# One pause before w2's shift, and a longer one for the sums of single tiles, in an eight-image attention and ConvNeXt kernel

## The chip, the cores and the metric

The kernel runs on one core of a Trainium2 chip, in float32. The metric is the device time of one execution, in microseconds (us). Before the change it is 3219.33 us, the median of three runs (3218.84 to 3219.62).

## The reference: what is computed

Eight images of 384 channels and 32 x 32 pixels go through two blocks.

```python
# layer 0, tokens: (8, 1024, 384)
xn = layernorm(xf, g1, beta1)
q, k, v = split_heads(xn @ w_qkv.T + b_qkv)          # 8 heads of 48
attn = softmax((q @ k.T) * 48 ** -0.5)
x1 = (attn @ v) @ w_proj.T + b_proj + xf
h = gelu(layernorm(x1, g2, beta2) @ w_fc1.T + b_fc1) # 1536 wide, exact gelu
x = x1 + h @ w_fc2.T + b_fc2
# layer 1
y = depthwise_conv_7x7(x) + dw_b
y = layernorm(y, ln_w, ln_b) @ w1 + b1               # 1536 wide
y = gelu(y)
nx = norm_over_pixels(y) / (mean_over_channels(norm_over_pixels(y)) + 1e-6)
y = grn_gamma * (y * nx) + grn_beta + y
x = x + y @ w2 + b2
```

## The kernel before, in words

The images are worked through one after the other. Image 0 goes through layer 0; from then on an image's layer 0 is interleaved with the previous image's layer 1 (the convolution, its layer norm, its two products).

Scores and weighted values of attention are taken in steps: for each half of the queries and each of four head pairs, eight steps of four small matmuls `s` (line 818), an exponential on ACT (827), and four matmuls `o` (838). The pair of PSUM tiles `o` of a head pair is emptied by `average` (lines 772 to 805): a copy on ACT (777), an addition on VectorE (779), the sums sent by SP (783), a reciprocal on VectorE (786), two trips through memory on SP, and a multiplication on VectorE (805). The projection (760) needs all four averages of its half; the second layer norm follows it: means by TensorE (518), subtraction (561), squares on ACT (568) and their sums on VectorE (572, 575), variance by TensorE (518 again).

The larger products (q and k, fc1, fc2, w1, w2) are done with fewer matmuls, on sums and differences of blocks of the weights and of the data. For this the sums of the weights are made once, while image 0 is worked on:

- `sums_singly` (1587 to 1640) loads 15 single tiles (960 KB) by POOL into a spare part of another buffer, waits, makes 18 small sums on VectorE (14 in line 1600, two in 1603, one each in 1637 and 1638), and stores the tiles by POOL (1640). Two chains `sums_for_tiles` do this three times each, for q and k's weights, for w1 and for w1 again, with a pause of 8.0 after each; `sums_for_fc1` does it twice for fc1.
- `forms` makes the sums of larger blocks for fc2 and later for w2 (lines 1651, 1654, 1683, 1692, 1694 on VectorE, loads 1661 and stores 1669 on POOL). Its buffer has the tag `acc`.
- `shift_through_w2` (1742 to 1763) works out what the GRN's `grn_beta` adds through w2, in three rounds. Each asks POOL for two loads of w2 (1746) into the buffer with the tag `acc`, multiplies them by `grn_beta` on VectorE (1752, twice), adds them up (1755, and 1759 five times), takes the column sum by TensorE (294) and adds the bias on ACT (1763). The tile is the one that `forms("fc2")` has used, so its load comes after the last stores from there.
- `prepare(weights, False)` does `forms("fc2")`, then `shift_through_w2`, then `forms("w2")`.
- On POOL and VectorE, lines 1725 to 1730 make a similar sum for w1's shift, in `pad`.

Each engine takes its instructions in the order in which the program writes them. That order is decided by the class `Flow` (137 to 173): all side work is written as generators, which yield a pause in microseconds of TensorE work. Whenever the main loop writes matmuls it calls `flow.pe(us)`, and the chains whose pause is over write their next instructions at this point. A longer pause so moves instructions behind others in the queues of their engines; nothing waits for a time on the chip. `pause()` holds back the sums on VectorE while the list `quiet` isn't empty, which is near the end of each half of the attention. Chains that have not ended are written out whole by `flow.finish` at certain points (2095 to 2113).

fc2 (1049 to 1145) takes its products in a chain with VectorE: differences and sums of `hid` and `fc_e` (1083) feed TensorE's matmuls (496), and VectorE (1080, 1083) adds the products to `x`.

Of the kernel before, what the change touches and what calls it, by code (L numbers as in the profile page):

```python
# [176 lines left out]
def block_kernel(  # L177
# [90 lines left out]
    def col(name, i):  # L268
        at, width = VEC[name]
        assert i < width  # L270
        return vec[:, at + i : at + i + 1]
# [20 lines left out]
    def column_sums(ps, i, weights, rows=slice(0, P)):  # L292

        nc.tensor.matmul(out=ps[rows, i : i + 1], lhsT=weights, rhs=ones[:, 0:1], start=True, stop=True)
        flow.pe(0.2)
# [13 lines left out]
    def columns(name):  # L309
        at, width = VEC[name]  # L310
        return vec[:, at : at + width]
# [38 lines left out]
    def chunk(w, c):  # L350
        return w[:, c * 6 * P : (c + 1) * 6 * P]
# [1230 lines left out]
    def pause():  # L1582
        for _ in range(24):
            if quiet:
                yield 1.0

    def sums_singly(w, store, spare):

        shape = store.shape
        t = spare[:, : shape[1] * shape[2] * P].rearrange("p (g n o) -> p g n o", n=shape[2], o=P)
        nc.gpsimd.dma_start(out=t, in_=w.rearrange("p (g n o) -> p g n o", n=shape[2], o=P))
        yield 9.0
        yield from pause()
        r = {n: t[:, :, i, :] for i, n in enumerate(SINGLY)}
        a12, a13, a21, a22, a23, a31, a32, a33 = (r[n] for n in (12, 13, 9, 4, 14, 0, 3, 10))

        def plus(dst, one_, other, op=ALU.add):
            nc.vector.tensor_tensor(dst, one_, other, op)  # L1600

        def minus(dst, one_, other):
            nc.vector.scalar_tensor_tensor(dst, one_, -1.0, other, ALU.mult, ALU.subtract)

        plus(r[6], r[6], a12)
        plus(r[14], a23, a33)
        yield 0.6
        yield from pause()
        minus(r[5], r[6], a33)
        plus(r[8], r[6], a13)  # L1610
        yield 0.6
        yield from pause()
        plus(r[8], r[8], r[14], ALU.subtract)
        plus(r[11], r[14], a12, ALU.subtract)
        yield 0.6
        yield from pause()
        plus(r[13], a13, a12, ALU.subtract)
        plus(r[13], r[13], a33, ALU.subtract)
        yield 0.6
        yield from pause()  # L1620
        plus(r[7], r[14], a22, ALU.subtract)
        plus(r[4], a21, a22)
        yield 0.6
        yield from pause()
        plus(r[2], a33, r[4], ALU.subtract)
        plus(r[4], r[4], a31)
        yield 0.6
        yield from pause()
        plus(r[1], a32, r[4])
        minus(r[9], a21, a12)  # L1630
        yield 0.6
        yield from pause()
        plus(r[9], r[9], a31, ALU.subtract)
        plus(r[0], a31, r[6], ALU.subtract)
        yield 0.6
        yield from pause()
        nc.vector.tensor_scalar(r[12], a12, -1.0, None, ALU.mult)
        nc.vector.tensor_scalar(r[14], r[14], -1.0, None, ALU.mult)
        yield 1.0
        nc.gpsimd.dma_start(out=store, in_=t)  # L1640

    def prepare(weights, aside):
# [3 lines left out]
        def blocks(name):  # L1646
            t = one.tile([P, CT, N], F32, tag="acc", name=name).rearrange("p c n -> p (c n)")
            return t.rearrange("p (j k o) -> p j k o", j=4, o=P)
# [93 lines left out]
        def shift_through_w2():  # L1742
            for r in range(CT):
                t = blocks(f"w2_gbeta_{r}")
                for s in range(2):
                    nc.gpsimd.dma_start(out=t[:, s], in_=chunk(w2, 2 * r + s).rearrange("p (k o) -> p k o", o=P))
                yield 14.0
                h = HT // 2
                for s in range(2):
                    yield from pause()  # L1750
                    g = columns("gbeta")[:, s * h : (s + 1) * h].unsqueeze(2).to_broadcast((P, h, P))
                    nc.vector.tensor_tensor(t[:, s], t[:, s], g, ALU.mult)
                    yield 1.0
                yield from pause()
                nc.vector.tensor_tensor(t[:, 0], t[:, 0], t[:, 1], ALU.add)
                for k in range(1, h):
                    yield 0.5
                    yield from pause()
                    nc.vector.tensor_tensor(t[:, 0, 0, :], t[:, 0, 0, :], t[:, 0, k, :], ALU.add)
                yield 7.0  # L1760
                ps = ps_s.tile([P, N], F32, tag="s", name=f"b2_{r}")
                column_sums(ps, 0, t[:, 0, 0, :])
                nc.scalar.activation(b2[:, r : r + 1], ps[:, :1], AF.Identity, bias=col("b2", r), scale=1.0)
# [7 lines left out]
        def release():  # L1771
            yield 14.0
            weights.release()

        yield from forms("fc2", wfc2, s_fc2)
        flow.spawn(release())
        yield from shift_through_w2()
        yield from forms("w2", w2, s_w2)

# [86 lines left out]
    def main():  # L1866
# [81 lines left out]
        def sums_for_tiles(i):  # L1948
            width = len(FORMS) * P
            spare = large[0][:, (2 * NP + 2 * i) * N : (2 * NP + 2 * i + 2) * N]  # L1950
            for w, store, g in ((wqkt, s_qk, i), (w1t, s_w1, i), (w1t, s_w1, i + 2)):
                yield from sums_singly(w[:, g * width : (g + 1) * width], store[:, g : g + 1], spare)
                yield 8.0

        def sums_for_fc1():
            width = len(FORMS) * P
            spare = v.rearrange("p t w -> p (t w)")
            for g in range(2):
                yield from sums_singly(wfc1t[:, g * width : (g + 1) * width], s_fc1[:, g : g + 1], spare)
                yield 8.0  # L1960
            for t in range(KT):
                nc.gpsimd.memset(v[:, t, :], 1.0)
# [122 lines left out]
        for b in range(B):  # L2085
            if b == 0:
                folding = flow.spawn(after(None, folds(weights), 8))
                preparing = flow.spawn(after(None, prepare(weights, False), 4))
                singly = [flow.spawn(after(None, sums_for_tiles(i), 33 + 5 * i)) for i in range(2)]
                aside = flow.spawn(after(folding, prepare(weights, True), 4))  # L2090
# [4 lines left out]
            if b == 0:  # L2095
                for chain in singly:
                    flow.finish(chain)
                fc1_sums = flow.spawn(after(None, sums_for_fc1(), 22.0))
                shift = flow.spawn(after(None, prepare(weights, None), 4.0))
# [204 lines left out]
```

## Time and profile before

| what | value |
|---|---|
| median of three runs | 3219.33 us |
| the profiled execution's own time | 3214.05 us |
| its span | 3212.3 us |
| mean granted TensorE clock | 0.999 |
| TensorE busy | 3197.8 us |
| VectorE busy | 2552.1 us |
| ACT busy | 1673.5 us |
| POOL busy | 493.2 us |
| moved by DMA | 393.09 MB, mean 122 GB/s |

The span runs from the first to the last event of the profiled execution; its own time is 1.75 us longer. Busy times are those of each engine's own instructions, and engines run beside each other. In a timeline a row has the start, the duration, the engine, the line of the kernel and the operation, and in brackets how long the engine was idle ahead of it and what ended that. In a list of waits a row has the waiting engine and line, what released it, the sum, the count and the longest in us.

### The profile page before, as it was taken

The numbers are of one execution on the slowest core, as the hardware profiler recorded it, in microseconds if no ns is written. First come the engines' busy times: TensorE is split into PE (matmuls) and PEld (weight loads), VectorE is DVE, ScalarE is ACT, GpSimd is POOL, SyncE is SP. The second block draws the span as 40 slices with busy tenths as digits, with TensorE's granted clock in tenths as the row PEclk, the third lists the DMA queues.
The fourth block names the chain that finished last, engine by engine and source line by source line (L and its number), as shares of the span: only waits on it lengthen the run. The fifth ranks groups of instructions, "written<-read, shape, count | busy, mean of one in ns | idle before, by whom it ended". The sixth has DMA issues, their size and how long they took to land.

```text
span 3212.3 us, 39348 instructions
## 1 busy us (share of the span) xinstructions
PE 3197.8 (100%) x14204; PEld 1398.9 (44%) x14204; DVE 2552.1 (79%) x3587; ACT 1673.5 (52%) x2363; POOL 493.2 (15%) x592
## 2 busy tenths in 40 slices
PE   9999999999999999999999999999999999999999
PEld 5344434443444434444344443444435444344454
DVE  4447788897878978789787888788888788879964
ACT  3442663456644476444754537637365374732543
POOL 2102221112111121201112011120111201200000
PEclk9999999999999999999999999999999999999999
DMA  6525742657336564456545374463743638433244
GB/s 212 173 94 177 172 92 50 159 115 163 81 87 160 120 156 92 93 146 151 119 92 123 116 185 102 81 136 106 192 93 81 147 98 200 73 81 93 54 120 111
DMA packets 206052, 393.09 MB, mean 122 GB/s; under 512 B 42656, under 2 KB 48416, under 8 KB 205472
## 3 DMA queue, kind: packets, MB, share of 16 engines
q0 software_dynamic: 79296, 163.35, 26.6%
q1 hardware_dynamic: 126272, 226.49, 23.5%
q8 instruction: 114, 1.87, 0.2%
q10 hardware_dynamic: 288, 0.71, 0.1%
q14 instruction: 82, 0.67, 0.1%
HBM read 212.98 MB, written 40.11 MB: 79 GB/s over the span
## 4 chain that ended last, share of the span: by engine, by line
PE 95%; DMA 1%; DVE 1%; issue 0%; ACT 0%; SPq 0%; POOL 0%; DVEq 0%; ACTq 0%; POOLq 0%
PE fc L415 15%; PE s L818 13%; PE o L838 12%; PE fc_p L496 11%; PE o_p L496 11%; PE proj L760 4%; PE v L738 3%; PE h_n L467 3%; PE h_z L467 3%; PE h_x L467 3%; PE h_last L1427 2%; PE o L1378 2%; PE h L402 2%; PE qk_n L467 2%; PE qk_z L467 2%; PE qk_x L467 1%
## 5 line engine op out<-in xcount | busy, mean ns | idle before, releaser
L1244 DVE SCALAR_TENSOR_TENSOR acc<-pad,vec,acc 128x870 f32<-128x870 f32 (+8 forms) x815 | 912.3, 1161 | 2.7
L827 ACT ACTIVATE p<-s 128x1024 f32<-128x1024 f32 x512 | 523.7, 1024 | 266.6 <-PE s L818 258.3
L838 PE MATMUL o<-p,v 64*64 64x512 f32 x4096 | 540.5, 589 | 4.0 <-DVE attn L779 4.0
L818 PE MATMUL s<-qk 48*64 48x512 f32 x4096 | 542.5, 591 | 0.2 <-ACT qk L660 0.2
L1280 POOL DMA_DIRECT2D acc<-tap x266 | 226.9, 859 | 1355.0 <-ACT tap L1279 668.3
L415 PE MATMUL fc<-xn,fc 128*128 128x512 f32 x972 | 427.5, 594 | 0.0
L496 PE MATMUL o_p<-y,w 128*128 128x512 f32 x664 | 289.0, 593 | 0.0
L838 PEld LDWEIGHTS o<-p,v 64*64 64x64 f32 x4096 | 165.3, 132 | 282.4 <-issue 269.6
L415 PEld LDWEIGHTS fc<-xn,fc 128*128 128x128 f32 x972 | 183.1, 190 | 228.7 <-issue 221.5
L818 PEld LDWEIGHTS s<-qk 48*64 48x64 f32 x4096 | 161.8, 132 | 277.4 <-issue 214.8
L496 PE MATMUL fc_p<-qk,fc 128*128 128x512 f32 x520 | 226.1, 593 | 0.0
L1279 ACT ACTIVATE tap<-pad,vec 128x512 f32<-128x512 f32 x266 | 195.1, 736 | 3.2 <-DMA acc<-tap 3.1
L496 PEld LDWEIGHTS o_p<-y,w 128*128 128x128 f32 x664 | 125.6, 190 | 157.7 <-issue 146.4
L1244 DVE SCALAR_TENSOR_TENSOR acc_last<-pad,vec,acc_last 128x377 f32<-128x377 f32 (+24 forms) x288 | 177.3, 694 | 0.6
L496 PEld LDWEIGHTS fc_p<-qk,fc 128*128 128x128 f32 x520 | 98.3, 190 | 126.1 <-issue 117.1
L508 ACT ACTIVATE qk<-fc,bfc_f 128x512 f32<-128x512 f32 x90 | 61.6, 684 | 160.7 <-PE fc L415 160.7
L508 ACT ACTIVATE hid<-fc,bfc_f 128x512 f32<-128x512 f32 x72 | 49.3, 686 | 159.4 <-PE fc L415 159.4
L760 PE MATMUL proj<-attn,wproj_sb 128*128 128x512 f32 x288 | 129.0, 602 | 2.1 <-DVE attn L805 2.1
L779 DVE TENSOR_TENSOR attn<-o,attn 128x512 f32<-128x512 f32 x64 | 44.1, 689 | 104.4 <-ACT attn L777 102.9
L738 PE MATMUL v<-wv_sb,xn 128*128 128x384 f32 x384 | 126.8, 487 | 0.0
L991 ACT COPY pad<-x 128x512 f32<-128x512 f32 x42 | 26.4, 635 | 185.3 <-DVE x L1083 185.3
L738 PEld LDWEIGHTS v<-wv_sb,xn 128*128 128x128 f32 x384 | 72.5, 190 | 50.1 <-issue 3.3
(446 smaller groups left out, 4601.5 us busy)
## 6 DMA issues: line engine op xcount, KB each, us to landing
acc<-tap POOLq DMA_DIRECT2D x266, 256.0 KB, 3.6
fc<-s_fc SPq DMA_DIRECT2D x91, 256.0 KB, 4.6
w<-s_w SPq DMA_DIRECT2D x91, 256.0 KB, 2.7
w<-s_w SPq DMA_DIRECT2D x72, 320.0 KB, 4.2
fc<-in_wfc SPq DMA_DIRECT2D x54, 384.0 KB, 3.9
y<-y POOLq DMA_DIRECT2D x38, 512.0 KB, 6.7
qk<-qk POOLq DMA_DIRECT2D x30, 512.0 KB, 9.5
qk<-s_qk SPq DMA_DIRECT2D x42, 320.0 KB, 4.7
```

The costliest lines, as they stand in the source:

```text
L415: nc.tensor.matmul(out=ps, lhsT=lhsT(k), rhs=rhs(k)[:, half(h)], start=(k == 0), stop=(k == nk - 1))
L467: nc.tensor.matmul(out=at, lhsT=weights.at(wname, g, slot // 5)[:, slot % 5, :], rhs=rhs[n], start=first, stop=True, skip_group_check=not ...
L496: nc.tensor.matmul(out=bank, lhsT=lhsT, rhs=rhs, start=k == 0, stop=k == len(pairs) - 1)
L508: nc.scalar.activation(dst, src, function, **kw)
L738: nc.tensor.matmul(out=ps[:, :C], lhsT=xn[:, k, t * P : (t + 1) * P], rhs=wv_sb[:, k, :], start=(k == 0), stop=(k == CT - 1),)
L760: nc.tensor.matmul(out=ps, lhsT=wproj_sb[:, m, ct * P : (ct + 1) * P], rhs=attn[:, m, :], start=(m == 0), stop=(m == CT - 1),)
L818: nc.tensor.matmul(out=s[64 * i : 64 * i + 64, j, :], lhsT=kT[64 * j : 64 * j + HD, m, k0 : k0 + 64], rhs=qT[64 * j : 64 * j + HD, m, half ...
L827: nc.scalar.activation(p, s, AF.Exp)
L838: nc.tensor.matmul(out=outs[i][64 * j : 64 * j + 64, :], lhsT=v[keys, t, at : at + 64], rhs=p[keys, j, :], start=(t == 0), stop=(t == KT - 1),
L1244: nc.vector.scalar_tensor_tensor(dst, window, tap, dst, ALU.mult, ALU.add)
L1279: nc.scalar.mul(t.rearrange("p (h w) -> p h w", w=W), window, tap)
L1280: nc.gpsimd.dma_start(out=acc[:, ct, half(h)], in_=t, accum_op=ALU.add)
```

## The change

The pause between asking for a group of 15 single tiles and the first sum on them becomes 13.0 where it was 9.0, in all eight uses. And between `forms("fc2")` and the shift through w2 there is a pause of 8.0 where there was none; `forms("w2")`, which comes after the shift in the same chain, is written later by the same. No instruction is added or removed.

```diff
@@ -1591,7 +1591,7 @@
         nc.gpsimd.dma_start(out=t, in_=w.rearrange("p (g n o) -> p g n o", n=shape[2], o=P))
-        yield 9.0
+        yield 13.0
         yield from pause()
@@ -1774,6 +1774,7 @@
         yield from forms("fc2", wfc2, s_fc2)
         flow.spawn(release())
+        yield 8.0
         yield from shift_through_w2()
         yield from forms("w2", w2, s_w2)
```

## The prediction

> **What bounds the kernel now.** I read the page first: TensorE is busy 3197.8 of 3212.3 us, so all that any change can take out of idle time is 14.5 us. The chain of work that ended last says the same.
>
> ```profile
> PE 3197.8 (100%) x14204; PEld 1398.9 (44%) x14204; DVE 2552.1 (79%) x3587; ACT 1673.5 (52%) x2363; POOL 493.2 (15%) x592
> ...
> PE 95%; DMA 1%; DVE 1%; issue 0%; ACT 0%; SPq 0%; POOL 0%; DVEq 0%; ACTq 0%; POOLq 0%
> ```
>
> Next, TensorE's waits in 0 to 420 us (waiting line, what released it, total, times, longest). Two of them are large, both in image 0's attention, both on VectorE:
>
> ```profile
> PE o L838 <- DVE attn L779: 4.0, 1, 4.0
> PE proj L760 <- DVE attn L805: 2.1, 1, 2.1
> ```
>
> The timeline says why (start, duration, instruction, idle before and releaser):
>
> ```profile
> 101.37 0.54 POOL L1669 DMA_DIRECT2D s_fc<-fc_b  x1 [0.19 <-issue]
> 106.74 1.08 POOL L1746 DMA_DIRECT2D w_gbeta<-in_w  x2 [4.83 <-issue]
> 107.81 1.06 POOL L1593 DMA_DIRECT2D qk<-in_w1t  x2
> ...
> 115.80 0.50 DVE L1600 TENSOR_TENSOR qk<-qk 128x128 f32<-128x128 f32 x2 [9.58 <-DMA qk<-in_w1t]
> 128.19 0.68 DVE L779 TENSOR_TENSOR attn<-o,attn 128x512 f32<-128x512 f32 x1
> ...
> 128.93 0.79 PE L838 MATMUL o<-p,v 64*64 64x512 f32 x2 [4.04 <-DVE attn L779]
> 145.99 7.97 PE L760 MATMUL proj<-attn,wproj_sb 128*128 128x512 f32 x14 [2.06 <-DVE attn L805]
> ```
>
> POOL asks for w2's first tile and has to sit 4.83 us until fc2's last stores have left it; behind it in POOL's queue stand the loads of w1's single tiles. VectorE reaches the sums of those tiles (L1600) 9.58 us early, and behind them stands L779, which frees the PSUM pair of head pair 1. Its ACT half was done at 110.2, yet it starts at 128.19. TensorE stops for it, and everything later in the averages is late, so the first projection stops for L805 as well.
>
> Cut on a grid of 3.413 us, the table of windows (busy us and count of PE, PEld, DVE, ACT, POOL, then granted clock) shows a second price:
>
> ```profile
> 122.50:125.94 3.44, 2.38 (x20) 0.59 (x12) 3.37 (x12) 2.46 (x3) 0.00 (x0) 1.00 0.20 35
> 125.94:129.35 3.41, 0.42 (x4) 0.21 (x8) 3.38 (x10) 0.00 (x0) 0.59 (x1) 0.99 0.34 142
> 129.35:132.76 3.41, 3.41 (x20) 1.07 (x16) 0.89 (x3) 0.38 (x1) 0.55 (x1) 0.51 0.41 149
> ...
> 143.00:146.42 3.42, 1.36 (x4) 0.40 (x3) 0.69 (x1) 0.00 (x0) 0.00 (x0) 0.99 0.66 172
> 146.42:149.83 3.41, 3.41 (x5) 1.35 (x4) 0.75 (x1) 0.00 (x0) 0.00 (x0) 0.51 0.87 319
> ```
>
> After the windows with 2.99 and 2.06 us idle the clock is 0.51 for one whole window; after one with 1.06 idle it isn't.
>
> **The skill.** The Trainium skill, "TensorE: Matmul & The Clock Gate", Part 1: The HAM clock gate, states a clock of 4/8 or 8/8 of full rate, decided on a free-running window of 3413 ns; an idle window throttles. The trace agrees, with 0.51, and adds that a window 60% idle is enough. The same page's table gives VectorE a strictly first-in, first-out queue; the trace agrees, L779 waiting 18 us behind work it doesn't need. "Trainium Kernel Development and Optimization", Key Constraints, says that DMAs of all queues share 16 engines; so an earlier load could crowd others. Here the busiest stretch near the change (110 to 120 us) has a DMA share of 0.89.
>
> **The change, part by part.** The instructions of both builds are the same in kind and number; SP's order is the same, TensorE and ACT exchange a few, VectorE and POOL are reordered, all in image 0. So nothing is added to any engine's work and the question is only which waits vanish and appear. From image 1 on a shift should carry to the end.
>
> What is removed. The first stall: the pair of L838 would have run on from 124.29, and ran at 128.93: 4.64 us. Its half-rate window: 100 matmuls took 13.02 instead of 10.75: 2.27 us. The projection: from 141.95 its 18 matmuls, at the 0.429 each of the second projection, should have ended at 149.67 and ended at 153.94: 4.27, of which about 2 is the clock. Together 11.2 us. In the new order VectorE has the six operations on `pad` (3.7 us) and then at once L779, at about 112 (after the reciprocal at 106.0 plus 1.7 that it slips), not 128.19; no operation on a late load is ahead of it. I followed the averages on: L805 of the last pair is done at 133.6 to 135.1, and TensorE needs it at 136.8. POOL issues w1's first load at about 104, w2's two at 107.5 and w1's second at 108.6; all have landed by 116, and are used from 145 on. So the whole 11.2 should be freed; low end 9, if the averages' DMAs are 2 us slower.
>
> What is moved, first place (A): the second layer norm's variance of half 0. Behind the first projection VectorE works without a pause up to L575, and TensorE's L518 needs that.
>
> ```profile
> 166.81 0.69 DVE L575 TENSOR_TENSOR ln_sq<-ln_sq,ln_sq 128x512 f32<-128x512 f32 x1
> ...
> 168.41 1.10 PE L518 MATMUL ln_var<-ln_sq,ones 128*128 128x512 f32 x2
> ```
>
> From the projection's end (153.96), L575 ends after 13.5 us and L518 starts after 14.45. In the new order eleven more operations precede L575: eight of 128x128 at 0.2 to 0.235 spacing (1.7 to 1.9) and two L1752 and one L1755 at 0.87 (2.6), so it ends after 18.0. TensorE comes half a step later (0.86) without w2's column sum (-0.24), and some 0.65 late because the squares on ACT wait for L561: 15.7. Stall 2.4, loss with the 0.65 3.0. Ends: 0, if VectorE makes good the 2.4 in ACT's gaps, and 5.0, with a half-rate window of 2.0. I take 3.0.
>
> Second place (B): fc2's partial products in image 0. Six sums of w2's blocks (L1651, L1654, L1683) run now while VectorE has nothing to do, ahead of the first L1080:
>
> ```profile
> 272.81 1.29 DVE L1654 TENSOR_TENSOR w_a<-w_a 128x512 f32<-128x512 f32 x2 [2.29 <-DMA w_a<-in_w]
> ...
> 276.08 0.69 DVE L1683 SCALAR_TENSOR_TENSOR w_y<-w_a 128x512 f32<-128x512 f32 x1
> 281.91 0.75 DVE L1080 SCALAR_TENSOR_TENSOR x<-fc_p,vec,x 128x512 f32<-128x512 f32 x1 [5.15 <-PE fc_p L496]
> ...
> 295.45 3.60 PE L496 MATMUL fc_p<-fc_e,fc 128*128 128x512 f32 x8
> ```
>
> They last 272.81 to 276.69, 3.9 us; in the new order they stand among L1080 and L1083, which feed TensorE. `fc_e` is done at 294.97 now, needed at 295.6; in the new order (before's clock) at 298.3, needed at 296.0. With 0.4 at the product before, the loss is 2.8. Ends: 0, if another operation has slack, and 4.8 with a half-rate window. I take 2.8.
>
> Costed at nothing: the load time of 13 for 9 (eight jobs, all ended before TensorE needs their stores; cover: SP's loads of them come an image later; uncovered, up to 4 us a job); column sums on TensorE moved (0.24 each, same number); the second half's averages (margin 2.2 us) and the second half of the layer norm (margin 3, left 2).
>
> Sum: -11.2 + 3.0 + 2.8 = -5.4 on the profiled execution's 3214.05 us (span 3212.3 and 1.75 around it), which lies 5.3 under the median. Carried over as it is: 3219.33 - 5.4 = 3213.9.
>
> **Rivals.** One, A and B hidden wholly or mostly: the layer norm's squares and fc2 have margins of 1.0 and 0.63 us today, and my spacings may be off by half. Then 8 to 11.2 us gain: 3208.1 to 3211.3. For it: a VectorE row costs its spacing, not its duration, and I may have counted a wait of ACT twice. Against: the operations do precede L575 and L1083 in order.
>
> Two, A and B hold and both bring a half-rate window: 11.2 - 3.0 - 2.8 - 4.0 = 1.4, so 3217.9. For it: an idle of 2.06 in one window sufficed; against: the grid can cut a stall of 2.4 in two.
>
> Three, slower: VectorE's lateness in fc2 persists through further products instead of being absorbed. To cancel the gain B must cost 8.2 instead of 2.8, for 0.2% slower 14.6: five products each 2.9 late, 3225.8 or more. It decides once VectorE's lateness at `fc_e` exceeds 8 us; the moved work is 3.9, so I think it unlikely.
>
> Four, the change doesn't do it: L779 still ends behind a landing. Then 3219. The built order speaks against it.
>
> **How the numbers follow.** The likeliest is A and B as worked: 0.42, and with my error of 2 us on it, 0.15 of that lies over 0.2% (6.4 us, about what a measurement can tell from no change). Rival one 0.36; two 0.10; three 0.08; four 0.04. Faster 0.15 + 0.36 = 0.51, same 0.27 + 0.14 = 0.41, slower 0.08. The range runs from all of the gain, 3207.5, to no gain, 3219.5; what lies outside is rival three and half of four, and a little below.
>
> **What would show it.** Right: no L779 or L805 among TensorE's waits before 150 us, no clock of 0.5 near 130 and 147; L779 of pair 1 at about 112. A: a wait of L518 on L575 near 158 of about 2.4 us. B: a wait of L496 on L1083 near 287 of about 2.3. Wrong if those are absent (time near 3208), if each is followed by a window at 0.5 (near 3218), or if image 1 shows a new wait.

## The result, and the profile after

The changed kernel takes 3212.17 us (3211.16 to 3213.08), the kernel before, run beside it, 3221.15 us (3218.5 to 3223.1): a ratio of 0.9973, interval 0.9964 to 0.9982, so 9.0 us or 0.27% faster. The prediction was 3213.9 with a range of 3207.5 to 3219.5.

The two profiled executions differ by much less: they took 3214.05 us before and 3213.02 after (spans 3212.3 and 3211.1). So there are two questions: where the predicted steps are in the trace, and where the other 8 us of the timed difference come from.

First, TensorE's waits of the changed kernel in 0 to 420 us (what waits, what released it, sum, count, longest):

```profile
PE fc_p L496 <- issue: 2.1, 1, 2.1
PE ln_var L518 <- DVE ln_sq L575: 2.1, 1, 2.1
...
PE proj L760 <- DVE attn L805: 0.7, 1, 0.7
PE fc_p L496 <- DVE hid L1083: 0.3, 1, 0.3
```

L779 is gone from the list, and L805 is down from 2.1 to 0.7, in the second half. In their place are the two that the prediction called A (L518) and B (the two of L496). Their rows in the timeline follow, ahead of them those of POOL and VectorE:

```profile
101.44 1.08 POOL L1746 DMA_DIRECT2D w_gbeta<-in_w  x2 [1.72 <-issue]
104.58 0.54 POOL L1593 DMA_DIRECT2D qk<-in_w1t  x1 [2.06 <-DMA s_qk<-qk]
...
109.79 0.69 DVE L779 TENSOR_TENSOR attn<-o,attn 128x512 f32<-128x512 f32 x1 [1.84 <-ACT attn L777]
...
133.91 0.69 DVE L805 TENSOR_TENSOR attn<-attn,r 128x512 f32<-128x512 f32 x1 [7.06 <-DMA r<-back]
...
160.35 1.12 PE L518 MATMUL ln_var<-ln_sq,ones 128*128 128x512 f32 x2 [2.08 <-DVE ln_sq L575]
...
288.87 1.99 PE L496 MATMUL fc_p<-hid,fc 128*128 128x512 f32 x4 [0.35 <-DVE hid L1083]
...
291.66 1.22 DVE L1083 TENSOR_TENSOR fc_e<-hid 128x1024 f32<-128x1024 f32 x1
292.98 3.74 PE L496 MATMUL fc_p<-fc_e,fc 128*128 128x512 f32 x8 [2.12 <-issue]
```

L779 of head pair 1 now follows ACT's copy at once, at 109.8 where it was at 128.2, and the last average of the half is done at 134.6, in time for the projection. The wait at 292.98 has no releaser in the list, but it reads `fc_e`, whose row on VectorE ends at 292.88, 0.1 us earlier.

The windows, cut on the changed kernel's grid of 3.413 us (busy us and count of PE, PEld, DVE, ACT, POOL, then clock, DMA share, GB/s):

```profile
155.22:158.63 3.41, 3.05 (x32) 0.78 (x22) 3.31 (x19) 2.52 (x3) 0.00 (x0) 1.00 0.02 1
158.63:162.04 3.41, 1.69 (x10) 0.65 (x14) 1.56 (x4) 0.52 (x1) 1.13 (x2) 1.00 0.63 252
162.04:165.45 3.41, 3.41 (x24) 0.80 (x13) 2.35 (x4) 2.40 (x4) 0.00 (x0) 0.50 0.79 324
...
288.32:291.73 3.41, 2.19 (x5) 0.68 (x4) 3.41 (x5) 0.59 (x1) 0.20 (x1) 1.00 0.55 213
291.73:295.14 3.41, 2.16 (x5) 0.98 (x6) 3.41 (x6) 0.00 (x0) 1.07 (x2) 1.00 0.44 139
```

Wait A falls nearly whole into one window, leaves it 1.69 us busy, and a window at 0.50 follows. Wait B is as long and is cut by the grid: two windows of 2.2 us busy each, and the clock stays full.

Matching the matmuls of both traces one by one, the changed kernel is 0.4 us ahead from the first 7 us on, and 10.8 us further at 143 us. It loses 4.8 by 203 us (A with its half-rate window), 1.1 by 210 (with the wait of the second half's projection for L805), 3.0 by 293 to 296 (B), and 1.3 in small steps in later images: 1.1 us are left at the end. The profiled executions therefore show the forecast terms, each near its size, with a net gain smaller than the forecast's 5.4. The timed runs gained more. That points at the profile of the kernel before.

### The profile page after: what moved, and what is told of

The parts are those of the page before. It is cut to its first block, busy times and chain, and to the rows that moved or that the text cites. A ratio compares the mean times of both kernels' runs of the same rounds, so it can differ in the third digit from the quotient of the medians.

```text
span 3211.1 us, 39348 instructions
## 1 busy us (share of the span) xinstructions
PE 3196.2 (100%) x14204; PEld 1402.1 (44%) x14204; DVE 2550.4 (79%) x3587; ACT 1674.6 (52%) x2363; POOL 493.4 (15%) x592
## 4 chain that ended last, share of the span: by engine, by line
PE 97%; DVE 1%; DMA 1%; ACT 0%; issue 0%; SPq 0%; DVEq 0%; ACTq 0%
PE fc L415 15%; PE s L818 13%; PE o L838 13%; PE o_p L496 11%; PE fc_p L496 11%; PE v L738 4%; PE proj L760 4%; PE h_n L467 3%; PE h_z L467 3%; PE h_x L467 3%; PE h_last L1427 2%; PE o L1378 2%; PE h L402 2%; PE qk_n L467 2%; PE qk_z L467 2%; PE qk_x L467 1%
## 5 line engine op out<-in xcount | busy, mean ns | idle before, releaser
L838 PE MATMUL o<-p,v 64*64 64x512 f32 x4096 | 535.7, 589 | 0.0
L496 PE MATMUL o_p<-y,w 128*128 128x512 f32 x664 | 289.0, 592 | 0.0
L838 PEld LDWEIGHTS o<-p,v 64*64 64x64 f32 x4096 | 166.4, 132 | 273.3 <-issue 265.0
L496 PE MATMUL fc_p<-qk,fc 128*128 128x512 f32 x520 | 226.6, 593 | 0.3 <-DMA qk<-qk 0.3
L496 PEld LDWEIGHTS o_p<-y,w 128*128 128x128 f32 x664 | 125.6, 190 | 157.7 <-issue 146.4
L496 PEld LDWEIGHTS fc_p<-qk,fc 128*128 128x128 f32 x520 | 98.2, 190 | 126.9 <-issue 117.4
L779 DVE TENSOR_TENSOR attn<-o,attn 128x512 f32<-128x512 f32 x64 | 44.1, 689 | 109.9 <-ACT attn L777 108.8
L760 PE MATMUL proj<-attn,wproj_sb 128*128 128x512 f32 x288 | 127.5, 596 | 0.7 <-DVE attn L805 0.7
```

The lines of the kernel that those rows point to most:

```text
L496: nc.tensor.matmul(out=bank, lhsT=lhsT, rhs=rhs, start=k == 0, stop=k == len(pairs) - 1)
L760: nc.tensor.matmul(out=ps, lhsT=wproj_sb[:, m, ct * P : (ct + 1) * P], rhs=attn[:, m, :], start=(m == 0), stop=(m == CT - 1),)
L838: nc.tensor.matmul(out=outs[i][64 * j : 64 * j + 64, :], lhsT=v[keys, t, at : at + 64], rhs=p[keys, j, :], start=(t == 0), stop=(t == KT - 1),
```

## The experiments

Theory S says that the time is set by these few waits of TensorE in image 0. Rival C says that these waits are not what sets the time; rival P, that the gain comes from the pause before the shift. Theory D, of the last experiment, says what makes the times of the kernel before spread. In each table and sentence below a time is the median of the timed runs, and a ratio is to the kernel before in the same series (3219.93 us for the first four, 3220.51 for the last three).

### The kernel before once more

> The kernel before, unchanged, to see how a second profile of it differs from the first (span 3212.3 us where its timed runs have a median of 3221.2). Theory S (the gain comes from TensorE's two waits in image 0's attention and what follows them): the waits of L838 on L779 (4.0) and of L760 on L805 (2.1) come again and are longer by up to several us in executions that take 3219 to 3223, since they start with a landing of DMA data; or more half-rate windows follow them. Rival C (the 9 us between the medians have nothing to do with these waits): the waits are again 4.0 and 2.1 us, and the time beyond 3212 us lies elsewhere. Time 3219 to 3223, ratio 1.000 +- 0.001.

Measured: 3218.78 us, ratio 0.9999 (0.9990 to 1.0007), single runs from 3216.9 to 3221.3; the 26 runs of the same kernel beside it from 3212.2 to 3222.7. The second profile has a span of 3215.0 us. From its timeline, TensorE's rows:

```profile
127.79 0.86 PE L838 MATMUL o<-p,v 64*64 64x512 f32 x2 [3.40 <-DVE attn L779]
...
148.08 8.20 PE L760 MATMUL proj<-attn,wproj_sb 128*128 128x512 f32 x14 [5.28 <-DVE attn L805]
```

and from the waits of SP's queue in 100 to 150 us:

```profile
SPq L799 <- DMA back<-inv: 3.7, 1, 3.7
```

POOL's and SP's timeline around it:

```profile
130.43 0.55 POOL L1593 DMA_DIRECT2D qk<-in_w1t  x1 [3.80 <-DMA s_w<-qk]
...
130.65 0.33 SPq L788 DMA_DIRECT2D back<-inv  x1
...
136.01 0.31 SPq L799 DMA_DIRECT2D r<-back  x1
```

The same three rows in the first profile:

```profile
131.56 0.55 POOL L1593 DMA_DIRECT2D qk<-in_w1t  x1 [3.80 <-DMA s_w<-qk]
...
131.78 0.33 SPq L788 DMA_DIRECT2D back<-inv  x1
...
133.48 0.52 SPq L799 DMA_DIRECT2D r<-back  x1
```

The same two waits are there as in the first profile, but L805's is 5.28 us instead of 2.06, and two half-rate windows in a row (145.2 to 152.0) go with it instead of one. One step earlier, SP's reading L799 comes 5.4 us after the 4 KB write `back<-inv`, where it was 1.7 us. In both executions POOL had issued 960 KB for the third group of single tiles 0.2 us ahead of that write, so that load is a suspect, not yet a cause. In the second execution the write landed at 135.94, 0.2 us after the load (135.76); in the first it landed at 133.19, well ahead of it (136.96). By the matching of matmuls the second execution falls 3.4 us behind the first at this projection and is 2.8 behind at the end. So S holds between these two, and the profile read for the prediction was a favourable one. The second is itself 2 to 4 us below the medians; no profile shows what the longer executions add.

The record also has the mean granted clock of every timed run. Of the 53 runs of the kernel before in the two series, the six at 0.999 took 3212.2 to 3218.1 us, the 40 at 0.998 took 3215.0 to 3222.7, and the seven at 0.997 took 3221.3 to 3223.5. One window at half rate lowers this mean by 0.0005 (an estimate, half of 3.413 us over 3212). So the longer executions are those with more time at half rate, which in the traces follows a long stall.

### Only the longer pause

```diff
-        yield 9.0
+        yield 13.0
```

> Only the longer pause (13 for 9), no pause before the shift. Built, VectorE has no sum of w1's tiles ahead of L779 of head pair 1, but L1752 twice and L1755 (2.6 us), behind w2's load that lands near 111. Theory S: L779 near 114 us, no wait of L838, at most 1 us of L805. The eleven added operations ahead of L575 lose the three of 0.87 us, so no wait A (2.1 in the changed kernel) and no half-rate window; the six block sums stay ahead of the first L1080, so no wait B (2.4). 4 to 7.5 us faster than the changed kernel: 3205 to 3208, ratio to before 0.995 to 0.996. Rival P (the pause before the shift is what brings the gain, since it lets POOL ask for w1's tiles 4 us earlier): the wait of L838 stays at 3 us or more, 3216 to 3221.

Measured: 3207.86 us, ratio 0.9965 (0.9951 to 0.9978). Rival P fails. This half of the change alone is faster than the whole, by 4.3 us between the medians and by 3.1 when each is set against the kernel before of its own series. L779 of head pair 1 is at 110.3 rather than near 114, since POOL asks for w2's tile at 102.0 (106.7 before) and VectorE is done with the two products and their sum at 109.2; L518 waits 0.43 us for L575; no window before the last few us is at half rate. One row was not foreseen. Here it is from the timeline, with its neighbour on POOL and what follows:

```profile
279.26 3.11 POOL L1962 MEMSET v<- 128x407 f32 x8
...
280.69 1.97 DVE L1692 TENSOR_SCALAR w_a<-w_a 128x512 f32<-128x512 f32 x1
...
286.97 2.34 DVE L1083 TENSOR_TENSOR fc_e<-hid 128x1024 f32<-128x1024 f32 x2
288.28 3.67 PE L496 MATMUL fc_p<-fc_e,fc 128*128 128x512 f32 x8 [1.10 <-ACT fc_n L1073]
```

L1692 takes 0.42 us in every other profile. It takes 1.55 longer here, and TensorE stops for 1.1 at the place where B is. The list names ACT's copy as the releaser, but that had ended at 287.8; the first of the two `fc_e` operations, which stand behind L1692 in VectorE's queue, ends at 288.18.

### Only the pause before the shift

```diff
+        yield 8.0
         yield from shift_through_w2()
```

> Only the pause of 8 before the shift; the load's pause stays 9. Built, 20 sums of w1's tiles stand ahead of L779 of head pair 1 again. Theory S: their load is asked for some 4 us earlier, so L779 is at about 121 instead of 128.2, still ahead of 124.3 where TensorE needs it: no wait of L838; but the averages behind it come 3 us later than in the changed kernel, so L760 waits for L805 for 3 to 4 us (0.7 in the changed one), perhaps with a half-rate window (1.7 to 2). Wait A about 0.5, wait B 2.4 as in the changed kernel. 3214 to 3218. Rival P: as fast as the changed kernel, 3211 to 3213.

Measured: 3217.10 us, ratio 0.9996 (0.9988 to 1.0004): no difference that can be told. TensorE's waits of this kernel:

```profile
PE proj L760 <- DVE attn L805: 6.1, 2, 5.2
PE fc_p L496 <- issue: 2.1, 1, 2.1
```

As S said, L838 no longer waits (L779 is at 122.6, ahead of 124), the projection does, and B is there. L805's waits are 0.9 and 5.2, both at this projection, where 3 to 4 was expected: SP's L799 waits 3.6 us for `back<-inv` again. The 960 KB are again issued 0.2 us ahead of it, and it lands 0.2 us after them (132.22 and 132.03). Two half-rate windows in a row go with it (140.9 to 147.7), and one follows B (297.9), which falls into one window this time. So the stall doesn't vanish with the POOL queue's order; it moves from L838 to L760. Rival P, the whole gain from this edit, fails here too.

### A without B

```diff
-            yield 16.0
+            yield 8.0 if name == "w2" else 16.0
```

> The changed kernel, with the pause of w2's sums of blocks after their load 8 for 16, so that the first block sums stand ahead of fc2's first L1080 again, in VectorE's 10 us of idle time there. Theory S: the two waits of L496 near 288 and 291 us (0.35 and 2.12) vanish, wait A of 2.1 stays; 3.0 us faster than the changed kernel, 3209.2 (3208 to 3210.5). Rival C: these waits are not what sets the time, 3212.

Measured: 3208.72 us, ratio 0.9967 (0.9954 to 0.9979). The waits of L496 are gone and that of L518 stays at 2.1. VectorE does the block sums, from 269.4 to 275.5, before L1080 at 276.0. For B, rival C fails: B costs about 3.5 us in the changed kernel. Of the six timed runs only the profiled one, the longest with 3210.09, has a mean clock of 0.999; the other five have 1.000. By the estimate above one window at half rate brings the mean down to 0.9995, just below what is listed as 1.000. So the half-rate window that follows A in this profile, as in that of the changed kernel, was most likely absent in those five.

### B without A

```diff
         yield from shift_through_w2()
+        yield 3.0
         yield from forms("w2", w2, s_w2)
```

with the pause of 13, and none before the shift.

> The longer pause of 13, no pause before the shift, and a pause of 3.0 between the shift and the sums of w2's blocks, with which VectorE's order in fc2 is that of the changed kernel. So B alone. Theory S: L518 waits about 0.4 as with the pause of 13 alone; the waits of L496 near 288 us (0.35 and 2.12) are back, 2 to 3 us slower than without B (3207.9 with the pause of 13 alone, which has a wait of 1.1 for L1073 in the same place): 3209 to 3211. Rival C: 3208 as without them, or 3212 as with A too.

Measured: 3209.19 us, ratio 0.9969 (0.9957 to 0.9980), L518 waiting 0.5, L496 2.1 and 0.4. Within what S expected.

### The memsets away from L1692

```diff
                 yield 8.0
+            yield 8.0
             for t in range(KT):
                 nc.gpsimd.memset(v[:, t, :], 1.0)
```

on top of the pause of 13 alone.

> As the pause of 13 alone, with a pause of 8 more before the eight memsets of v on POOL. There L1692 took 1.97 us beside these memsets and 0.42 in all other profiles, and TensorE waited 1.1 us for L1073 after it. Theory S: L1692 takes 0.42, no wait of L496 on L1073, 1 to 1.5 us faster than 3207.9: 3206.4 to 3207. Rival: L1692 is slow for another reason, and stays at 1.97 and 3207.9.

Measured: 3206.42 us (3205.3 to 3206.92), ratio 0.9958 (0.9944 to 0.9972). The row is back at its usual size:

```profile
280.26 0.42 DVE L1692 TENSOR_SCALAR w_a<-w_a 128x512 f32<-128x512 f32 x1
```

and no wait of L496 is left there. It is 1.4 us faster than without this edit, as 1.55 of delay and 1.1 of waiting let expect. This is the fastest version measured, some 5.8 us below the changed kernel (5.1 when each is set against its own kernel before); it has neither A nor B. So the four combinations can be set side by side:

| | without B | with B |
|---|---|---|
| without A | 3206.42 | 3209.19 |
| with A | 3208.72 | 3212.17 |

A is worth 2.3 to 3.0 us, B 2.8 to 3.5, both 5.75. The changed kernel is from another series than the other three, whose kernels before lie 0.6 to 1.2 us lower; that is the accuracy of the table.

### The kernel before, with the third load after the averages

```diff
+                late = 15.0 if g == 2 else 0.0
+                if late:
+                    yield late
+                    nc.vector.memset(spare[:, :1], 0.0)
-                yield from sums_singly(w[...], store[...], spare)
+                yield from sums_singly(w[...], store[...], spare, max(9.0 - late, 0.0))
```

where the arguments are shortened and the last one is the pause after the load. The load has to wait for the small memset, and VectorE comes to that after the last L805 of the half.

> The kernel before, with the load of the third group of single tiles (960 KB by POOL) put behind the last L805 of the first half, by a VectorE memset of one column of its tile (below 0.1 us); all other orders as before. In the second profile of the kernel before this load was issued 0.2 us ahead of the 4 KB write back<-inv, on which SP then waited 3.7 us, and L760 waited 5.3 instead of 2.1. Theory D (this load is what makes the times of before spread from 3212 to 3223): no wait of SP's L799 on back<-inv, L760 waits for about 2, times 3212 to 3216 with a spread below 3 us. Rival (the spread comes from elsewhere, the clock's grid or the store of 960 KB ahead of the load): median 3218 to 3220 with the same spread.

Measured: 3214.75 us, ratio 0.9982 (0.9975 to 0.9988), 5.8 us faster than the kernel before. SP no longer waits for `back<-inv` (L799 follows it by 1.7 and 2.7 us), and the projection waits 1.2 us. The store of 960 KB ahead of the load stays where it was, 4.6 us before the write, so the store alone did not hold it up here. But the times still spread over 6.8 us, from 3211.5 to 3218.2 (10.4 for the kernel before beside it), where less than 3 was expected. The profile shows where some of that may come from:

```profile
118.42 0.49 DVE L1600 TENSOR_TENSOR qk<-qk 128x128 f32<-128x128 f32 x2 [11.89 <-DMA qk<-in_w1t]
...
131.54 1.12 PE L838 MATMUL o<-p,v 64*64 64x512 f32 x2 [7.03 <-DVE attn L779]
```

In this execution the second group's load lands at 118.4, not 115.8, and L838 waits 7.0 instead of 4.0 (3.4 in the second profile of before). So D is right on the median and wrong on the size of the spread: this load is one source of it. In three executions the first stall was 4.0, 3.4 and 7.0 us long, and it ends later where the load lands later.

## Why the prediction was right, and where it was off

**What was removed, the first stall.** Right. L779 was put at about 112 and is at 109.8, the last L805 of the half ends at 134.6 (133.6 to 135.1 forecast), and neither wait nor half-rate window is left before 150 us. In the profiles 10.8 us were freed of 11.2. POOL's loads, forecast at about 104, 107.5 and 108.6, were asked for 4 to 6 us earlier, at 99.2, 101.4 and 104.6, which did no harm.

**A.** Right in place and mechanism: 2.08 us of L518 on L575 for 2.4 forecast (18.0 less 15.7 is in fact 2.3), and L575 ends 17.6 us after the projection for 18.0. The profile's loss is 4.8 with the half-rate window, between the 3.0 that was taken and the upper end of 5.0; in timed runs it is 2.3 to 3.0. A mean clock of 1.000 in four of the changed kernel's eleven timed runs, and in five of the six without B, speaks for executions in which no half-rate window follows A; no profile shows such an execution.

**B.** Right: 0.35 and 2.12 for 0.4 and 2.3, 3.0 us in the profile, 2.8 to 3.5 in the timed runs, 2.8 forecast (its parts add up to 2.7). No window at half rate here, since the grid cut the stall in two.

**What was costed at nothing.** The second half's averages, with a margin of 2.2 us, did bring a wait: 0.7 us of the projection for L805, and 1.1 of loss by 210 us. The versions with the longer pause alone and with the later memsets have it too (1.0 and 0.8). And the shift didn't carry whole to the end: 1.3 us were lost in later images, for causes that were not looked into.

**The rivals.** The hiding of A and B didn't occur: both are there. Two half-rate windows at once didn't occur in the profile, one did. No further products of fc2 were late. That the change doesn't do what it says is excluded by L779's time.

**The step that was off** is the sum, "Carried over as it is: 3219.33 - 5.4 = 3213.9". The 5.3 us by which the profile of before lay under the median were taken as an offset that any version has. The changed kernel doesn't have it: its profiled execution is 0.9 us above its median. The term mis-sized is the freed time. In timed runs it is 9.0 + 5.75 = 14.7 us, or, from the kernel before to the version with neither A nor B, 3220.5 - 3206.4 = 14.1, where 11.2 was read from one execution. The second profile and the kernel with the later third load show a part of the rest: the 960 KB of the third group, which in the old order are asked for in the middle of the averages, can hold up the 4 KB of sums' reciprocals by 3.7 us, and L805 with them. Asking for them later was worth 5.8 us in timed runs. Whether this is all of the rest is not shown. In the changed kernel the sums of the second groups are behind the projection, so their stores start at 158.7 and the third load behind those. That takes this load out of the averages. It doesn't take every such wait out: with the longer pause alone L799 still waits 2.6 us for `back<-inv`, at 118 to 123 us, but there the averages are early enough that TensorE doesn't wait. The prediction followed what each moved load would collide with in its new place, and did not ask what it had collided with in its old one, because in the execution at hand it happened to collide with nothing.

That the time came within 1.7 us of 3213.9, while the gain was mis-sized by 3.6, is in part luck: the median of the kernel before was 3219.33 in three runs and 3221.15 in eleven.

**The chances.** Faster had 0.51, same 0.41. The measured 0.27% is past the bound of 0.2%, by the mis-sized term: with 14.1 for 11.2, and A and B as taken, the sum would have been -8.3, near the measured -9.0.

**What the two edits do apart.** The prediction treated them as one. The longer pause brings the gain (12.1 us in its series), the pause before the shift puts three to four of its microseconds back, by A and B: it moves the shift's three large operations before L575, and with it w2's block sums out of VectorE's idle time.

## What to carry to other kernels

A wait that starts with a DMA landing can differ from execution to execution; here one was 4.0, 3.4 and 7.0 us, another 2.1 and 5.3. Before its length goes into a sum, compare the profile's own time with the median; where they differ by as much as the effect in question, take a second profile, and look at small transfers that are issued beside large ones, since such a one made the difference here. And when side work is moved to free one stall, count the operations that come to stand ahead of the next narrow margins (here 1.0 and 0.6 us) on the same engine: here A and B were most of the price. Two edits that were made together should be timed apart.

## What the runs showed of the hardware

- A TensorE window need not be idle as a whole for the next to be at half rate. Windows with 0.42, 1.36 and 1.69 us busy of 3.41 were followed by 0.5, windows with 2.16, 2.19 and 2.38 by full rate. One window near the end of the kernel with the pause before the shift alone (3209.5 us, 1.54 busy) was followed by full rate, so these figures give no exact bound. The Trainium skill ("TensorE: Matmul & The Clock Gate", Part 1: The HAM clock gate) speaks of an idle window; here about half an idle window sufficed in all but that one. So a stall of about 2.1 us costs 1.7 more (an estimate, half of 3.41) or nothing, by where the grid cuts it. B shows both: cut in two in the changed kernel, it was followed by full rate; in the kernel with the pause before the shift alone it fell into one window (294.5 to 297.9, 1.28 busy) and the next was at 0.50.
- A 128x512 TENSOR_SCALAR took 1.97 us beside memsets on POOL, 0.42 without, while TENSOR_TENSOR rows of 128x1024 beside such memsets kept their 1.2 us each. The Trainium skill ("GPSIMD Engine Reference", Specifications) says that GpSimd's SBUF interfaces are shared with VectorE, with contention for VectorE instructions in a 2-port mode or with two SBUF inputs. The first row agrees that there is contention, though no trace shows its mode. The rows with two inputs showed none, beside memsets (`v<-`), which have no input; no run here has them beside a POOL operation that reads.
- A write of 4 KB took SP 1.7 us until it could be read back, or 5.4 us when 960 KB had been issued by POOL 0.2 us earlier, in one execution and not in another of the same program; with the pause before the shift alone it was 5.3 us, behind such a load again. A load just ahead isn't the only occasion: with the longer pause alone one took 4.3 us (118.45 to 122.75), 6.5 us after POOL had asked for 960 KB. In these three late cases the write landed 0.2 us after a transfer that POOL had asked for earlier: 135.94 after 135.76, 132.22 after 132.03, and 122.67 after 122.51 (a store of `pad`). Why it was behind that transfer there, and ahead of it in the first profile, is open.
